# A four-layer graph network: the order of chunks in a tile of layer 0, and where the tile's end stands in the schedule

## The chip, the cores and the metric

The kernel runs on one core of a Trainium2 chip. Its time is the device time of one execution in microseconds (us); lower is better. The core has a matrix engine (TensorE, "PE" in the profile, with its weight loads as "PEld"), a vector engine (VectorE, "DVE"), a scalar engine (ScalarE, "ACT"), GpSimd ("POOL") and a queue that only issues transfers (SyncE, "SP"). Each engine takes its own instructions in a fixed order, and semaphores hold it where it needs another's result.

## The reference

Four graph layers run one after the other over 3125 nodes of 128 features and 100,000 edges, sorted by destination. Each layer's output is added to its input and normalized per node. Layer 0, which the change concerns most, is an attention over the edges that come into each node, with eight heads of 16 features, and with the node itself as one more neighbour:

```python
pre_edge = hP1[dst] + hP2[src] + zP3[edge_type]     # edge_type: one of 500 relations
logit_edge = _leaky(pre_edge) @ y_w                 # 128 -> 8 heads
alpha = ex / denom[dst_a]                           # softmax over a node's edges and itself
t_edge = hWh[src] + zWz[edge_type]
agg = jax.ops.segment_sum((alpha[:, :, None] * t).reshape(-1, D), dst_a, num_segments=n)
out = _leaky(agg + residual_weight * h)
```

Here hP1, hP2 and hWh are products of the node features with 128 x 128 weights, and zP3 and zWz are products of a table of 500 x 64 relation features. The self term also needs z_bar, the mean of the relation features of a node's edges. Layer 1 is a mean over neighbours with a small two-step network, layer 2 an attention with four heads and an edge bias, layer 3 an attention with typed nodes and edges.

## The kernel before

**Tiles, slots and chunks.** The nodes are sorted by degree and cut into 25 tiles of 128, one node per partition. A tile has CAP[t] edge slots per node (57 in tile 0, falling to 21), and `chunks(t)` cuts these into chunks of W = 8 slots and a shorter rest. A tile of the middle has five or four chunks. A prologue (`prologue`, L780 on) makes the node's own products hw and hq, and is issued for the next tile ahead of the last chunk of the present one.

**Two ways to do a chunk.** Both begin with eight gathers of neighbour rows from h_tab into a buffer hs (`gather`, L90, an indirect DMA on POOL; one gather brings one slot of all 128 nodes). hs has eight buffers.
- `gathered` (L819 on) also gathers eight rows of z_tab, the table of relation products, into a buffer zs, of which there are two. DVE adds zs to hs (L826), sums the relation features in halves (L814, L817) and adds them to the tile's sum (L828), after which zs is free. PE then forms the argument of the logits in PSUM (L799, L833), ACT applies the rectifier (L806), and PE multiplies with y_w (L808).
- `multiplied` (L838 on) gathers no zs. SP brings the relation numbers (L843), DVE makes one-hot matrices of them (L852), and PE multiplies these with the relation table (L854). ACT copies the result (zT, L856), PE forms the argument (L858, L860) and the value part (L866), which DVE adds to hs (L867). The relation features are summed from zT (L870, L874).

`by_matmul(t)` gives the first slots of the chunks that are multiplied. In a five-chunk tile they come as: multiplied, gathered, multiplied, gathered, gathered rest.

**The end of a tile.** `masked` (L881, L882) collects the logits of all chunks in lgs. `softmax` (L680 to L692) takes the maximum mx, the factor corr for what was summed earlier, the exponentials (ACT, L688) and their sum sm, and updates the running maximum m and the running sum l. `faded` (L697) scales the earlier sum ac. `spread` (L889, L814, L817, L891) multiplies the values of each chunk with the weights and sums them; when it is done with a chunk, that chunk's hs is free for a later gather. Then follow the self term, the output, the layer norm and the transfers out (L950 to L1008, with the scatter `put`, L93, on POOL). `softmax` is also used by layers 2 and 3, once per chunk there.

**Counts.** Layer 1 works with a table of how often each node is a neighbour of each other. `counts` (L562 to L645) makes this table from the edge lists on DVE, PE and ACT, during layer 0. It is a generator: after each chunk the loop takes some steps of it (`next(steps, None)`), so that the counts of all tiles are spread over layer 0. Only layer 1 reads the result (c_tab).

**What sets the order.** The program is written in plain order, and a scheduler puts the instructions of each engine in their final order. It takes what is ready by its own estimate of times, and among these prefers what has priority. Priority follows the order in the program, unless a block asks for more with `tc.high_priority(offset=...)`, which ranks the block that many places ahead. Pools decide when a buffer may be written again, in the order in which it was asked for: a gather into hs waits until the chunk eight chunks earlier was spread.

Of the kernel before, what the change touches and what calls it, by code (L numbers as in the profile page):

```python
# [8 lines left out]
F32 = mybir.dt.float32  # L9
# [3 lines left out]
AF = mybir.ActivationFunctionType  # L13
OP = mybir.AluOpType
AX = mybir.AxisListType
# [3 lines left out]
P = 128  # L19
N = 3125  # L20
NT = 25
# [6 lines left out]
W = 8  # L28
# [5 lines left out]
H = 8  # L34
# [6 lines left out]
CAP = [57, 42, 40, 39, 38, 37, 36, 35, 35, 34, 33, 33, 32, 31, 31, 30, 30, 29, 28, 28, 27, 26, 25, 24, 21]  # L41
assert len(CAP) == NT
OFF = [sum(CAP[:t]) for t in range(NT + 1)]
# [7 lines left out]
NB = [3] * 3 + [2] * (NT - 4) + [1]  # L51
CW = 512
NCW = -(-NP // CW)


def chunks(t):
    return [(s, min(W, CAP[t] - s)) for s in range(0, CAP[t], W)]
# [7 lines left out]
    return [(run[0][0], sum(run[-1]), run) for run in runs]  # L65


def by_matmul(t):

    full = CAP[t] // W  # L70
    n = (9 * CAP[t] + 10 * W) // (20 * W)
    return {i * full // n * W for i in range(n)}


@with_exitstack
def tile_gnn(ctx, tc, a, out):
    nc = tc.nc
    V, A, G, T = nc.vector, nc.scalar, nc.gpsimd, nc.tensor
# [400 lines left out]
    mask = late.tile([P, NS], F32, name="mask")  # L479
# [6 lines left out]
    with tc.tile_pool(name="srcp", bufs=1) as sp, tc.tile_pool(name="srcq", bufs=2, space=PSUM) as ps:  # L486
# [28 lines left out]
        for o in range(0, NS, P):  # L515
            n = min(P, NS - o)
# [158 lines left out]
    def softmax(pool, lg, n, heads, m, l, ex=None):  # L675


        ex = lg if ex is None else ex
        mx = pool.tile([P, heads], F32, name="mx")
        V.tensor_reduce(mx, lg.rearrange("p s h -> p h s"), AX.X, OP.max)  # L680
        mn = pool.tile([P, heads], F32, name="mn")
        V.tensor_max(mn, m, mx)
        corr = pool.tile([P, heads], F32, name="corr")
        V.tensor_sub(corr, m, mn)
        A.activation(corr, corr, AF.Exp)
        V.tensor_copy(m, mn)
        V.tensor_sub(lg, lg, mn.unsqueeze(1).to_broadcast([P, n, heads]))
        A.activation(ex, lg, AF.Exp)  # L688
        sm = pool.tile([P, heads], F32, name="sm")
        V.tensor_reduce(sm, ex.rearrange("p s h -> p h s"), AX.X, OP.add)  # L690
        V.tensor_mul(l, l, corr)
        V.tensor_add(l, l, sm)  # L692
        return corr

    def faded(acc, corr, heads):
        acch = acc.rearrange("p (h d) -> p h d", h=heads)
        V.tensor_mul(acch, acch, corr.unsqueeze(2).to_broadcast([P, heads, D // heads]))  # L697
# [56 lines left out]
    with tc.tile_pool(name="l0", bufs=2) as wp, tc.tile_pool(name="l0s", bufs=1) as sp, \  # L754
# [4 lines left out]
        m = sp.tile([P, NT, H], F32, name="m")  # L759
# [77 lines left out]
        def multiplied(hq, o, n, zbT, first, lg_ps):  # L837

            hs = wp.tile([P, W, HC], F32, name="hs", bufs=8)
            for s in range(n):  # L840
                gather(hs[:, s, :], h_tab, srcx[:, o + s:o + s + 1])
            rb = wp.tile([P, W * P], F16, name="rb")
            nc.sync.dma_start(rb[:, :n * P], rel_tab[o:o + n].rearrange("(o s) p -> o (s p)", o=1)  # L843
                              .to_broadcast([P, n * P]))
            zT = wp.tile([P, W * P], F32, name="zT")
            for s0 in range(0, n, 4):
                k = min(4, n - s0)
                cols = slice(s0 * P, (s0 + k) * P)
                oh = wp.tile([P, NK, 4 * P], BF16, name="oh")[:, :, :k * P]
                zps = ps1.tile([P, 4 * P], F32, name="zps")[:, :k * P]  # L850
                for i in range(NK):
                    V.tensor_scalar(oh[:, i], rb[:, cols], relid[:, i:i + 1], None, op0=OP.is_equal)  # L852
                    for k2 in range(2):
                        T.matmul(zps, zq[:, i, 2 * R * k2:2 * R * (k2 + 1)], oh[:, i], start=(i + k2 == 0),  # L854
                                 stop=(i == NK - 1 and k2 == 1))
                A.activation(zT[:, cols], zps, AF.Copy)  # L856
                pre = argument(hq, k)
                T.matmul(pre[:, :k], zw[:, :D], zT[:, cols], start=False, stop=False)  # L858
                for s in range(k):
                    T.matmul(pre[:, s, :], hs[:, s0 + s, :D], ident, start=False, stop=(s == k - 1))  # L860
                logits(pre, k, lg_ps[:, s0:s0 + k])
            for s0 in range(0, n, 3):
                k = min(3, n - s0)
                t_ps = ps1.tile([P, 3, HC - D], F32, name="t_ps")
                for s in range(k):
                    T.matmul(t_ps[:, s, :], zT[:, (s0 + s) * P:(s0 + s + 1) * P], zw[:, D:], start=True, stop=True)  # L866
                V.tensor_add(hs[:, s0:s0 + k, D:], hs[:, s0:s0 + k, D:], t_ps[:, :k])  # L867
            assert n == W
            zh = wp.tile([P, W // 2, P], F32, name="zh")
            V.tensor_add(zh, zT.rearrange("z (s p) -> z s p", p=P)[:, :W // 2],  # L870
                         zT.rearrange("z (s p) -> z s p", p=P)[:, W // 2:])
            halved(zh, W // 2, zbT if first else None)
            if not first:
                V.tensor_add(zbT, zbT, zh[:, 0])  # L874
            return hs

        def masked(lg_ps, hss, n, mk):

            lg = wp.tile([P, max(CAP), H], F32, name="lgs")
            for s0, w, hs in hss:  # L880
                V.tensor_add(lg[:, s0:s0 + w], lg_ps[:, s0:s0 + w], hs[:, :w, 2 * D:])  # L881
            V.tensor_add(lg[:, :n], lg[:, :n], mk.unsqueeze(2).to_broadcast([P, n, H]))  # L882
            return lg

        def spread(ac, hs, ex, n):

            val = hs[:, :n, D:2 * D]
            valh = val.rearrange("p s (h d) -> p s h d", h=H)
            V.tensor_tensor(valh, valh, ex.unsqueeze(3).to_broadcast([P, n, H, D // H]), op=OP.mult)  # L889
            halved(hs[:, :, D:2 * D], n)  # L890
            V.tensor_add(ac, ac, hs[:, 0, D:2 * D])  # L891
# [25 lines left out]
        for t in range(NT):  # L917
# [5 lines left out]
            lg_ps = ps1.tile([P, max(CAP), H], F32, name="lg")  # L923
            zbT = wp.tile([P, P], F32, name="zbT")
            hss = []
            mults = by_matmul(t)
            for s0, w in chunks(t):
                o = OFF[t] + s0
                if s0 + w == n and t + 1 < NT:

                    ahead = x_next, prologue(t + 1, x_next)
                if s0 in mults:
                    hs = multiplied(hq, o, w, zbT, s0 == min(mults), lg_ps[:, s0:s0 + w])
                else:
                    hs = gathered(hq, lambda s: srcx[:, o + s:o + s + 1], rel[:, o:o + w], w, za, lg_ps[:, s0:s0 + w])
                hss.append((s0, w, hs))

                done += n_steps * w / NS
                while done > 0:
                    next(steps, None)  # L940
                    done -= 1
            lg = masked(lg_ps, hss, n, mask[:, OFF[t]:OFF[t + 1]])
            corr = softmax(wp, lg[:, :n], n, H, m[:, t, :], l[:, t, :])
            faded(ac, corr, H)
            for s0, w, hs in hss:
                spread(ac, hs, lg[:, s0:s0 + w], w)


            zaT_ps = ps1.tile([P, P], F32, name="tp", tag="misc")
# [420 lines left out]
```

## Time and profile before

| | |
|---|---|
| Time, median of 3 runs | 4817.54 us (4814.24 to 4825.97) |
| Profiled execution, its own time | 5636.56 us |
| Its span in the profile | 5634.8 us |
| Mean granted TensorE clock | 0.619 of full |
| Busy in the span: POOL, DVE, PE, ACT | 54%, 53%, 36%, 16% |
| Preparation | 0 to about 204 us |
| Layer 0 | about 204 to 2850 us |
| Layer 1 | about 2850 to 3060 us |
| Layer 2 | about 3060 to 4400 us |
| Layer 3 | about 4400 to 5635 us |

The profile is of one execution, which was 819 us longer than the median of the runs without a profile. Durations come from it, and totals are to be set against its own time. A row of the groups names line, engine, operation, tile written and tiles read, count, busy time and mean duration, and then the idle time of the engine just before these instructions with what ended it. "issue" as a cause means that nothing in the profile shows a wait, and "remote" an update whose sender the trace doesn't tell.

### The profile page before, as it was taken

What the parts mean: (1) busy time and instruction counts of PE and PEld (TensorE: products, weight loads), DVE (VectorE), ACT (ScalarE), POOL (GpSimd) and SP (SyncE); (2) the same over time, 40 slices, a digit from 0 to 9 for tenths busy, and PEclk for the clock granted to TensorE, in tenths of its full rate; (3) what the DMA queues carried; (4) which work ended last, traced back from release to release, by engine and by line L of the source; (5) the groups of instructions that cost most, each with busy time, mean ns of one, the idle gap of its engine ahead of it and who ended that gap; (6) DMA issues with size and microseconds to landing.
All of it is one profiled execution on the core that took longest, in us unless ns stands there. A gap on an engine that the chain in (4) does not pass through costs nothing. (4 is left out here: it accounts for less than half of the span.)

```text
span 5634.8 us, 37936 instructions
## 1 busy us (share of the span) xinstructions
PE 2025.8 (36%) x10974; PEld 1311.2 (23%) x11061; DVE 2959.0 (53%) x6784; ACT 927.9 (16%) x2462; POOL 3069.7 (54%) x3137
## 2 busy tenths in 40 slices
PE   7164554556544555555564022222233100000000
PEld 5143433334333444334432010111111000000000
DVE  8354664555544655555432455555566354555555
ACT  1032222222222322222111011111111000000000
POOL 0545566454554445444503756666564476666665
PEclk9576766666676777776677555555555555555555
DMA  2423333332233333323343333333332233333322
GB/s 82 124 73 91 93 93 96 86 90 75 77 91 84 83 86 88 89 82 84 101 170 119 105 96 105 104 103 114 98 109 84 81 100 91 89 89 95 94 85 68
DMA packets 220244, 530.70 MB, mean 94 GB/s; under 512 B 65689, under 2 KB 112460, under 8 KB 215385
## 3 DMA queue, kind: packets, MB, share of 16 engines
q0 software_dynamic: 147968, 437.97, 27.6%
q1 hardware_dynamic: 72024, 89.90, 4.9%
q8 instruction: 94, 1.54, 0.1%
q14 instruction: 158, 1.29, 0.1%
HBM read 457.09 MB, written 70.63 MB: 94 GB/s over the span
## 5 line engine op out<-in xcount | busy, mean ns | idle before, releaser
L90 POOL DMA_INDIRECT hs<-h_tab,srcx x821 | 880.3, 1072 | 666.2 <-issue 534.7
L90 POOL DMA_INDIRECT kv<-kv_tab,pay_sb x821 | 783.6, 954 | 423.9 <-issue 241.1
L90 POOL DMA_INDIRECT kv<-ktv_tab,pay_sb x821 | 780.2, 950 | 336.0 <-issue 256.1
L90 POOL DMA_INDIRECT zs<-z_tab,rel x445 | 458.0, 1029 | 451.6 <-DVE az L828 141.6
L706 DVE TENSOR_REDUCE u<-msg 128x128 f32<-128x1024 f32 (+4 forms) x228 | 384.3, 1686 | 114.5 <-remote 61.6
L808 PE MATMUL lg<-yw,low 128*128 128x8 f32 x1642 | 243.5, 274 | 126.2 <-ACT low L806 72.2
L634 PE MATMUL c_ps<-c_ohs,c_ohd 128*128 128x128 bf16 x1300 | 139.5, 264 | 406.3 <-issue 193.9
L808 PEld LDWEIGHTS lg<-yw,low 128*128 128x128 f32 x1642 | 235.5, 218 | 173.0 <-ACT low L806 107.1
L1315 DVE TENSOR_TENSOR qk<-kv,qp 128x1024 f32<-128x1024 f32 (+4 forms) x114 | 126.5, 1110 | 279.4 <-DMA kv<-ktv_tab,pay_sb 257.4
L559 DVE TENSOR_TENSOR c_ohs<-c_ends,c_up 128x1024 bf16<-128x1024 bf16 (+4 forms) x178 | 113.2, 637 | 296.1 <-remote 251.0
L612 ACT ACTIVATE c_oha<-c_oha,srclo 128x50 bf16<-128x50 bf16 (+2 forms) x821 | 201.4, 327 | 355.6 <-DVE c_oha L608 270.1
L854 PE MATMUL zps<-oh,zq 128*128 128x512 bf16 x677 | 237.7, 466 | 49.4 <-DVE oh L852 21.4
L702 DVE TENSOR_TENSOR msg<-kv,ex 128x1024 f32<-128x1024 f32 (+4 forms) x228 | 249.3, 1105 | 0.0
L866 PE MATMUL t_ps<-zw,zT 128*128 128x136 f32 x752 | 153.3, 340 | 212.9 <-DVE hs L867 128.2
L1163 DVE TENSOR_TENSOR qk<-kv,qp 128x1024 f32<-128x1024 f32 (+4 forms) x114 | 126.1, 1107 | 183.2 <-DMA kv<-kv_tab,pay_sb 175.6
L634 PEld LDWEIGHTS <-c_ohd 128*128 128x128 bf16 x1300 | 114.0, 118 | 431.8 <-issue 333.0
L799 PE MATMUL pre<-identb,hq 128*128 128x512 bf16 (+3 forms) x645 | 203.3, 414 | 5.0 <-issue 4.1
L636 ACT ACTIVATE c_sb<-c_ps 128x512 bf16<-128x512 f32 (+1 forms) x175 | 96.3, 550 | 653.8 <-remote 441.9
L717 PE MATMUL tp<-ident,xk 128*128 128x128 f32 x100 | 43.6, 436 | 432.7 <-DVE xk L1231 131.2
L806 ACT ACTIVATE low<-pre 128x512 f32<-128x512 f32 (+1 forms) x215 | 123.1, 574 | 406.3 <-remote 140.3
L826 DVE TENSOR_TENSOR hs<-hs,zs 128x2112 f32<-128x2112 f32 (+7 forms) x67 | 132.6, 1979 | 102.9 <-issue 43.8
L866 PEld LDWEIGHTS t_ps<-zw,zT 128*128 128x128 f32 x752 | 130.1, 234 | 239.2 <-DVE hs L867 137.5
(398 smaller groups left out, 5183.8 us busy)
## 6 DMA issues: line engine op xcount, KB each, us to landing
c_tab<-c_sb SPq DMA_DIRECT2D x25, 768.0 KB
cs<-c_tab SPq DMA_DIRECT2D x6, 3200.0 KB
hs<-h_tab,srcx POOLq DMA_INDIRECT x821
kv<-kv_tab,pay_sb POOLq DMA_INDIRECT x821
kv<-ktv_tab,pay_sb POOLq DMA_INDIRECT x821
rb<-rel_tab SPq DMA_DIRECT2D x47, 256.0 KB
zs<-z_tab,rel POOLq DMA_INDIRECT x445
h_tab<-h SPq DMA_DIRECT2D x25, 132.0 KB
```

The source lines that it names most:

```text
L90: return G.indirect_dma_start(out=dst, out_offset=None, in_=table, in_offset=indirect(idx), **kw)
L612: A.activation(oha[:, s, 0, :], oha[:, s, 1, :], AF.Copy, scale=srclo[:, o:o + 1])
L634: T.matmul(cps[:, j * P:(j + 1) * P], ohd[:, b // 2, :, b % 2], ohs[:, b // 2, :, b % 2], start=(i == 0), stop=(i == nb - 1))
L702: V.tensor_tensor(msg[:, :n, :].rearrange("p s (h d) -> p s h d", h=heads), val.rearrange("p s (h d) -> p s h d", h=heads), ex.unsqueeze(3 ...
L706: V.tensor_reduce(u, msg[:, :n, :].rearrange("p s d -> p d s"), AX.X, OP.add)
L799: T.matmul(pre[:, :k], hq[:, i, :], identb.unsqueeze(1).to_broadcast([P, k, P]), start=(i == 0), stop=False)
L808: T.matmul(lg_ps[:, s, :], low[:, s, :], yw8, start=True, stop=True)
L826: V.tensor_add(hs[:, :n], hs[:, :n], zs[:, :n, :HC])
L854: T.matmul(zps, zq[:, i, 2 * R * k2:2 * R * (k2 + 1)], oh[:, i], start=(i + k2 == 0), stop=(i == NK - 1 and k2 == 1))
L866: T.matmul(t_ps[:, s, :], zT[:, (s0 + s) * P:(s0 + s + 1) * P], zw[:, D:], start=True, stop=True)
L1163: V.tensor_mul(qk[:, :n], kv[:, :n, :D], qp.unsqueeze(1).to_broadcast([P, n, D]))
L1315: V.tensor_mul(qk[:, :n], kv[:, :n, :D], qp.unsqueeze(1).to_broadcast([P, n, D]))
```

## The change

1. `by_matmul(t)` becomes `in_order(t)`. As many chunks are multiplied as before, now always the first ones by slot number, and the list alternates between gathered and multiplied chunks so that a multiplied one is last. The gathered chunks are taken from the end of the tile, so the short rest comes first. A five-chunk tile becomes: gathered rest, gathered, multiplied, gathered, multiplied. The prologue of the next tile is still issued ahead of the last chunk.
2. `softmax` is split. `weights` does what the values need, with the exponentials of the logits ahead of that of corr. `rest` does the copy of m, the sum sm and the update of l. In layer 0 `rest` comes behind the spreads; layers 2 and 3 still call both together, through `softmax`.
3. The tile's end, from `masked` to `rest`, is in a block with a priority of AHEAD = 600 places.
4. zbT, the sum of the multiplied relation features, is begun by the chunk with slot 0, which is the first multiplied one in the new order too.

```diff
--- before.py
+++ after.py
@@ -51,6 +51,7 @@
 NB = [3] * 3 + [2] * (NT - 4) + [1]
 CW = 512
 NCW = -(-NP // CW)
+AHEAD = 600
 
 
 def chunks(t):
@@ -65,11 +66,14 @@
     return [(run[0][0], sum(run[-1]), run) for run in runs]
 
 
-def by_matmul(t):
-
-    full = CAP[t] // W
+def in_order(t):
+
+
     n = (9 * CAP[t] + 10 * W) // (20 * W)
-    return {i * full // n * W for i in range(n)}
+    mult = [(s, w, True) for s, w in chunks(t)[:n]]
+    rest = [(s, w, False) for s, w in chunks(t)[n:]][::-1]
+    k = len(mult) + len(rest)
+    return [(mult if (i + 1) * n // k > i * n // k else rest).pop(0) for i in range(k)]
 
 
 @with_exitstack
@@ -675,6 +679,12 @@
     def softmax(pool, lg, n, heads, m, l, ex=None):
 
 
+        corr, rest = weights(pool, lg, n, heads, m, l, ex)
+        rest()
+        return corr
+
+    def weights(pool, lg, n, heads, m, l, ex=None):
+
         ex = lg if ex is None else ex
         mx = pool.tile([P, heads], F32, name="mx")
         V.tensor_reduce(mx, lg.rearrange("p s h -> p h s"), AX.X, OP.max)
@@ -682,15 +692,18 @@
         V.tensor_max(mn, m, mx)
         corr = pool.tile([P, heads], F32, name="corr")
         V.tensor_sub(corr, m, mn)
-        A.activation(corr, corr, AF.Exp)
-        V.tensor_copy(m, mn)
         V.tensor_sub(lg, lg, mn.unsqueeze(1).to_broadcast([P, n, heads]))
         A.activation(ex, lg, AF.Exp)
-        sm = pool.tile([P, heads], F32, name="sm")
-        V.tensor_reduce(sm, ex.rearrange("p s h -> p h s"), AX.X, OP.add)
-        V.tensor_mul(l, l, corr)
-        V.tensor_add(l, l, sm)
-        return corr
+        A.activation(corr, corr, AF.Exp)
+
+        def rest():
+            V.tensor_copy(m, mn)
+            sm = pool.tile([P, heads], F32, name="sm")
+            V.tensor_reduce(sm, ex.rearrange("p s h -> p h s"), AX.X, OP.add)
+            V.tensor_mul(l, l, corr)
+            V.tensor_add(l, l, sm)
+
+        return corr, rest
 
     def faded(acc, corr, heads):
         acch = acc.rearrange("p (h d) -> p h d", h=heads)
@@ -923,14 +936,14 @@
             lg_ps = ps1.tile([P, max(CAP), H], F32, name="lg")
             zbT = wp.tile([P, P], F32, name="zbT")
             hss = []
-            mults = by_matmul(t)
-            for s0, w in chunks(t):
+            todo = in_order(t)
+            for i, (s0, w, mult) in enumerate(todo):
                 o = OFF[t] + s0
-                if s0 + w == n and t + 1 < NT:
+                if i + 1 == len(todo) and t + 1 < NT:
 
                     ahead = x_next, prologue(t + 1, x_next)
-                if s0 in mults:
-                    hs = multiplied(hq, o, w, zbT, s0 == min(mults), lg_ps[:, s0:s0 + w])
+                if mult:
+                    hs = multiplied(hq, o, w, zbT, s0 == 0, lg_ps[:, s0:s0 + w])
                 else:
                     hs = gathered(hq, lambda s: srcx[:, o + s:o + s + 1], rel[:, o:o + w], w, za, lg_ps[:, s0:s0 + w])
                 hss.append((s0, w, hs))
@@ -939,11 +952,14 @@
                 while done > 0:
                     next(steps, None)
                     done -= 1
-            lg = masked(lg_ps, hss, n, mask[:, OFF[t]:OFF[t + 1]])
-            corr = softmax(wp, lg[:, :n], n, H, m[:, t, :], l[:, t, :])
-            faded(ac, corr, H)
-            for s0, w, hs in hss:
-                spread(ac, hs, lg[:, s0:s0 + w], w)
+
+            with tc.high_priority(offset=AHEAD):
+                lg = masked(lg_ps, hss, n, mask[:, OFF[t]:OFF[t + 1]])
+                corr, rest = weights(wp, lg[:, :n], n, H, m[:, t, :], l[:, t, :])
+                faded(ac, corr, H)
+                for s0, w, hs in hss:
+                    spread(ac, hs, lg[:, s0:s0 + w], w)
+                rest()
 
 
             zaT_ps = ps1.tile([P, P], F32, name="tp", tag="misc")
```

## The prediction

> **What bounds the kernel now.** I read the page first, for the costliest rows.
>
> ```profile
> PE 2025.8 (36%) x10974; PEld 1311.2 (23%) x11061; DVE 2959.0 (53%) x6784; ACT 927.9 (16%) x2462; POOL 3069.7 (54%) x3137
> ...
> L90 POOL DMA_INDIRECT hs<-h_tab,srcx x821 | 880.3, 1072 | 666.2 <-issue 534.7
> ...
> L90 POOL DMA_INDIRECT zs<-z_tab,rel x445 | 458.0, 1029 | 451.6 <-DVE az L828 141.6
> ```
>
> Both rows belong to layer 0, and POOL issues them one after the other. The timeline of POOL shows the step in an undisturbed stretch: 0.95 us busy, 0.30 between, one gather each 1.25 us. Layer 0 has 821 + 445 + 25 indirect DMAs (the 25 are L93), so its floor on POOL is 1291 x 1.25 = 1614 us. It lasts from about 204 to 2850 us: 2646 us. The view by stretches says that no engine is full there:
>
> ```profile
> 204.00:1200.00 996.00, 514.34 (x3228) 375.77 (x3255) 502.98 (x1239) 251.75 (x685) 570.24 (x540) 0.68 0.34 91
> 1200.00:1400.00 200.00, 111.38 (x621) 78.92 (x628) 89.34 (x235) 47.75 (x136) 102.04 (x97) 0.65 0.30 81
> 1400.00:2850.00 1450.00, 791.23 (x4844) 559.68 (x4884) 767.46 (x2201) 366.95 (x969) 723.95 (x705) 0.70 0.31 85
> ```
>
> Columns: length, busy us of PE, PEld, DVE, ACT and POOL, then clock, DMA share, GB/s. So layer 0 is bound by waits between engines. Those of POOL, layer 0 only:
>
> ```profile
> POOL hs L90 <- issue: 534.7, 773, 38.4
> POOL zs L90 <- DVE az L828: 141.6, 14, 19.3
> ...
> POOL x_tab L93 <- DVE x L735: 79.5, 7, 36.0
> ```
>
> "issue" here is mostly one long wait a tile plus 0.30 per gather: 773 waits, 534.7 us, so about 773 x 0.30 = 232 of stepping and 300 of real waiting. What ends a long one is seen where tile 9's end meets tile 10's fourth chunk, POOL above, DVE below:
>
> ```profile
> 1507.89 0.95 POOL L90 DMA_INDIRECT zs<-z_tab,rel  x1 [19.10 <-DVE az L828]
> 1532.62 5.77 POOL L90 DMA_INDIRECT hs<-h_tab,srcx  x1 [23.78 <-issue]
> ```
>
> ```profile
> 1497.71 2.35 DVE L826 TENSOR_TENSOR hs<-hs,zs 128x2112 f32<-128x2112 f32 x1
> ...
> 1516.32 0.69 DVE L881 TENSOR_TENSOR lgs<-lg,hs 128x64 f32<-128x64 f32 x5
> ...
> 1524.10 1.51 DVE L593 TENSOR_REDUCE c_pos<-c_inc 128x32 f32<-128x800 f32 x1
> 1525.53 0.16 DVE L692 TENSOR_TENSOR l<-l,sm 128x8 f32<-128x8 f32 x1
> 1525.60 1.22 DVE L889 TENSOR_TENSOR hs<-hs,lgs 128x1024 f32<-128x1024 f32 x1
> ...
> 1531.60 0.28 DVE L891 TENSOR_TENSOR az<-az,hs 128x128 f32<-128x128 f32 x1
> ```
>
> The hs gather starts 0.7 us after L891 of the old tile's first chunk ends: it had waited for an hs buffer. Between the L826 add of the NEXT tile's first gathered chunk (1497.7) and that release (1531.9) DVE does the tile end mixed with count work (L559, L589, L593). All long gaps of 1 us or more add up in layer 0 to some 898 us: hs 425, zs 320, the rest put and x.
>
> The profiled execution took 5636.6 us, 819 more than the median 4817.5. Many waits in it end "remote" (ACT c_sb L636 441.9 us, DVE c_ohs L559 251.0), so they are partly the recording's. Were all 819 us in layer 0, it would really last 1827; were they spread evenly, 2261. I take 2050, so 2050 - 1614 = 436 us of real POOL waiting (range 210 to 650). All sums below are differences made on profile durations and put on the median.
>
> **What the Trainium skill says.** "Perfetto Trace Analysis", Optimization Strategy: a bubble that repeats on the engine that should be saturated can mean too few buffers for the next tile. The trace agrees: 38.4, 26.4, 23.8, 34.1, 24.4 us on consecutive tiles, each at the ninth hs buffer. The same page, DMA Instruction — SWDGE (GPSIMD): the recorded end of a GpSimd DMA is the end of descriptor generation, and the data lands later. No row here gives that landing time, so it is part of an 8.5 us allowance below. "SBUF — State Buffer", the box on SWDGE: a DVE operation in a two-port mode can keep GpSimd from writing descriptors. The 5.77 us gather above fits, beside DVE's spread; nothing here proves it. DVE's amount of work does not change, so I give it nothing.
>
> **The change, part by part.**
>
> Order of chunks: a five-chunk tile goes from M G M G r to r G M G M (M multiplied, G gathered, r the short gathered rest). Gathers stay 821 + 445, multiplied chunks 47 of 114, DVE work of tiles 1 to 23 goes 1236 to 1243 us. Nothing is bought in work; only positions move. I laid both programs' queues side by side. The tile's own last gather now stands 35 to 55 gathers ahead of the first one that needs its buffers (16 to 49 before). That would pay, but in both queues the spread still stands on DVE behind the L826 add of the next tile's gathered chunk, so the cover counts from THAT chunk's last gather. In gathers, tiles 1 to 12: before 8 8 8 30 8 16 8 8 1 8 8 41; after 11 2 16 17 8 3 0 12 9 8 8 9. Four-chunk tiles 13 to 19: before 41 to 49; after 35 29 40 39 4 38 37.
>
> DVE from that gate to the release: mean 18.5 us before (6.4 of it counts), 16.1 after (4.8). The scheduler still mixes counts in: tile 8 goes from 23.0 to 30.1 us, 15.6 of it counts.
>
> Price per tile: max(0, gate-to-release + 8.5 - cover x 1.25). Tile 8: before 23.0 + 8.5 - 10 = 21.5 (the trace shows 26.4, so the model has about the right size); after 30.1 + 8.5 - 15 = 23.6. Tile 6: 23.2 + 8.5 - 20 = 11.7, after 25.3 + 8.5 - 3.8 = 30.0. Tile 3: 22.7 + 8.5 - 10 = 21.2, after 23.3 + 8.5 - 20 = 11.8. Tile 12: 27.7 + 8.5 - 51 is below 0, after 26.4 + 8.5 - 11 = 23.7. Done gather by gather, largest wait of each tile: hs 235 before, 263 after; zs (same rule, released by L828) 110 before, 94 after. Sum 345 against 357: +12 us. The allowance is my estimate; at 3 us the difference is -6, at 16 us +60. Scaled to the 436 us above (x 436/345): +15, from -8 to +76.
>
> weights/rest: the m copy (0.163), sm (0.618), two operations on l (0.157 each) go behind the spreads, about 1.1 us of DVE a tile off the release, 27 us over 25 tiles if each tile waits there; this is already in the 16.1. Exp of corr (206 ns) behind the other exp: under 0.2 us a tile. For layers 2 and 3 these are the same operations in another order, and u L706 and msg L702 fill DVE there beside kv gathers: 0, at most 228 x 0.16 = 36 us either way, if each chunk waited for it.
>
> high_priority by 600: no instruction added. Counts are put behind; they feed layer 1 only, at 2850, so hidden; uncovered they can cost up to one tile's share, 22 us. Queued behind a tile end placed early on DVE are the next chunk's L826 and L852, and so PE and the zs release. SP's rb loads go with their chunks: 47 before and after, none on the path.
>
> Sum: 4817.5 + 15 (stalls), and a few us for delayed count and put work (a guess between 0 and 22, taken as 7): 4840.
>
> **Rivals.**
> A, faster: the tile end really stops binding. If the spread comes out ahead of the next tile's L826 in time as well as in the queue, half of the hs waits go: 425/898 x 436 = 206, half 103, and 27 more from the shorter end: about 4690. For: the repeating bubble, the tile's own slack of 35 to 55 gathers (44 to 69 us). Against: the gate in the queue. It decides if the next tile's first gathered chunk lands before the last multiplied one of this tile is through PE.
> B, no change: DVE, PE and POOL are each so near the tile period that a wait taken from hs comes back at zs or x_tab: 4817.
> C, slower by more: the four-chunk tiles, which wait nowhere by my sum before, now have their buffers released late, and early-placed tile ends hold up L826. With a step of 1.0 us a gather instead of 1.25, less cover, the same sum gives 732 against 578, +154; half of it +77: 4895, up to 4970.
>
> **How the numbers follow.** A measurement of this kernel tells 0.3%, 14 us, from no change. Forecast, 4810 to 4895 with 4840 as its middle: 0.42 (faster 0.02, same 0.10, slower 0.30). A, 4690 to 4803: 0.30, faster. B: 0.08 (0.02 faster, 0.04 same, 0.02 slower). C, 4895 to 4970: 0.20, slower. Together faster 0.34, same 0.14, slower 0.52. The range leaves out the ends of A and C: 4705 to 4950; the forecast's own is 4810 to 4895.
>
> **What would show it.** Right: POOL hs waits per tile of 15 to 30 us still there in tiles 3 to 11, new ones in tiles 12 to 16 and 19, zs waits ended by L828 a little smaller, the L826 of the next tile ahead of L881 in DVE's timeline. Rival A: hs waits fall under 200 us and the tile period shrinks evenly. C: DVE waits ahead of L826 and x_tab grow. Wrong about layers 2 and 3: their stretches change length by over 20 us. What would make it all wrong: real waits that the recording hides, since it is 17% longer than the runs.

## The result

The changed kernel takes 4879.56 us (median of 4 runs, 4875.56 to 4883.56) where the kernel before takes 4818.69 (4 runs beside it). The ratio is 1.0125, with a 95% interval of 1.0107 to 1.0142: 61 us slower. The forecast was 4840, so its direction was right and its size too small by almost a factor of three (+22 of +61).

The profile of the changed kernel has a span of 4878.6 us, near its runs. That of the kernel before, on which the prediction rests, had 5634.8. So the kernel before was profiled once more (run before_again below); this second profile has 4814.1 us and is the one to compare with. From here on, "before" in comparisons of traces is this second profile. In some groups of runs the kernel before takes 5589 to 5643 us, without a profile too, for a reason that is open, so each result stands beside the time of the kernel before in its own group, and only groups with about 4819 us are compared with the result above.

Where the time goes is seen from when layers 1, 2 and 3 begin. The lines are from the view by tile (the matmuls of layer 1, the gathers of layers 2 and 3), with minimum, median and maximum duration in ns and then the first and last start in us. Kernel before, second profile:

```profile
L1113 PE MATMUL y_ps<-cs,u x513: 219/379/631, 2319.1 to 2457.8; 128*128 128x512 bf16 x146, 128*128 128x128 bf16 x25
L90 POOL DMA_INDIRECT kv<-kv_tab,pay_sb x821: 941/947/1616, 2508.8 to 3607.2; - x165
L90 POOL DMA_INDIRECT kv<-ktv_tab,pay_sb x821: 941/947/1142, 3692.4 to 4783.5; - x165
```

The changed kernel (its lines stand 4 to 16 further down):

```profile
L1129 PE MATMUL y_ps<-cs,u x513: 219/379/631, 2386.3 to 2524.7; 128*128 128x512 bf16 x146, 128*128 128x128 bf16 x25
L94 POOL DMA_INDIRECT kv<-kv_tab,pay_sb x821: 940/946/1578, 2576.3 to 3674.3; - x165
L94 POOL DMA_INDIRECT kv<-ktv_tab,pay_sb x821: 940/946/1111, 3758.0 to 4848.0; - x165
```

Layer 1 begins 67 us later, and the two steps after that are 190 and 1182 us long against 190 and 1184. All of the loss is in layer 0; the reordered softmax of layers 2 and 3 costs nothing.

The groups of the page that answer to those shown before the prediction, changed kernel:

```profile
PE 1915.6 (39%) x10963; PEld 1273.4 (26%) x11061; DVE 2923.6 (60%) x6784; ACT 921.7 (19%) x2462; POOL 3167.7 (65%) x3137
...
L94 POOL DMA_INDIRECT hs<-h_tab,srcx x821 | 937.1, 1141 | 389.0 <-issue 269.8
...
L94 POOL DMA_INDIRECT zs<-z_tab,rel x445 | 498.2, 1120 | 194.1 <-issue 123.8
L839 DVE TENSOR_TENSOR hs<-hs,zs 128x2112 f32<-128x2112 f32 (+5 forms) x67 | 132.9, 1984 | 566.2 <-DMA zs<-z_tab,rel 480.6
```

and the second profile of the kernel before:

```profile
L90 POOL DMA_INDIRECT hs<-h_tab,srcx x821 | 919.0, 1119 | 380.9 <-issue 323.8
...
L90 POOL DMA_INDIRECT zs<-z_tab,rel x445 | 487.7, 1096 | 181.8 <-issue 124.2
L826 DVE TENSOR_TENSOR hs<-hs,zs 128x2112 f32<-128x2112 f32 (+7 forms) x67 | 132.9, 1984 | 498.5 <-DMA zs<-z_tab,rel 344.3
```

The same gathers are busy 18 + 11 us longer: no gather was added, but one takes 1141 and 1120 ns in the mean instead of 1119 and 1096. The idle time in front of them grew by 8 + 12 us. DVE sits 68 us longer in front of its add of zs, where it waits for the gathers of zs, and all that is queued on DVE behind this add waits too.

That suggests an account of layer 0 by POOL's timeline. From the first hs gather to the last hs or zs gather, the time is: 0.95 us for each of about 1311 DMAs and the small gaps between them (together 1642 us before and 1638 in the changed kernel), plus the **waits** (gaps of 1 us and more), plus the **excess** (what each of these DMAs lasts beyond 0.95 us). The **tail** is from the end of the last gather to the first matmul of layer 1.

| us | waits | excess | tail |
|---|---|---|---|
| before | 183 | 210 | 79 |
| changed | 204 | 244 | 95 |
| difference | +22 | +34 | +16 |

These three give 72, the small rest takes back some 4, and the start of layer 1 moved by 67. Half of the loss is thus not waiting at all, but gathers that last longer. The longest of the changed kernel, with the DVE rows at its end:

```profile
354.10 15.54 POOL L94 DMA_INDIRECT hs<-h_tab,srcx  x1 [5.32 <-issue]
```

```profile
367.94 0.28 DVE L904 TENSOR_TENSOR az<-az,hs 128x128 f32<-128x128 f32 x1
368.14 0.68 DVE L827 TENSOR_TENSOR hs<-hs 128x512 f32<-128x512 f32 x1
368.74 0.96 DVE L702 TENSOR_REDUCE sm<-lgs 128x8 f32<-128x456 f32 x1
```

During all of the 15.54 us DVE runs the spread. The gather ends at 369.64 us, 0.90 us after the start of the first DVE instruction behind it. If the excess of every DMA is laid over the DVE instructions that run from its start to 0.9 us before its end, 75 us of it before and 115 in the changed kernel fall on the spread; the add of zs (L826, L839 in the changed kernel) has 69 and 70. So the growth is the spread's.

### The profile page after: what moved, and what is told of

Same layout as the page of the kernel before. It is cut to its first block, busy times and chain, and to the rows that moved or that the text cites. A ratio compares the mean times of both kernels' runs of the same rounds, so it can differ in the third digit from the quotient of the medians.

```text
span 4878.6 us, 37948 instructions
## 1 busy us (share of the span) xinstructions
PE 1915.6 (39%) x10963; PEld 1273.4 (26%) x11061; DVE 2923.6 (60%) x6784; ACT 921.7 (19%) x2462; POOL 3167.7 (65%) x3137
## 4 chain that ended last, share of the span: by engine, by line
POOL 24%; issue 13%; DVE 6%; PE 5%; DMA 3%; ACT 1%; DVEq 0%; another core or an unknown queue 0%; SPq 0%; POOLq 0%; ACTq 0%
POOL kv L94 23%; PE y_ps L1129 2%; DVE msg L715 1%; DMA kv<-kv_tab,pay_sb 1%; DVE u L719 1%; DMA kv<-ktv_tab,pay_sb 1%; PE p_ps L1249 1%; DVE qk L1179 1%; PE e_ps L1257 1%; DVE qk L1331 1%; PE p_ps L1144 0%; POOL xqb L94 0%; POOL out L97 0%; POOL ktv_tab L97 0%; PE tp L730 0%
## 5 line engine op out<-in xcount | busy, mean ns | idle before, releaser
L94 POOL DMA_INDIRECT hs<-h_tab,srcx x821 | 937.1, 1141 | 389.0 <-issue 269.8
L94 POOL DMA_INDIRECT zs<-z_tab,rel x445 | 498.2, 1120 | 194.1 <-issue 123.8
L839 DVE TENSOR_TENSOR hs<-hs,zs 128x2112 f32<-128x2112 f32 (+5 forms) x67 | 132.9, 1984 | 566.2 <-DMA zs<-z_tab,rel 480.6
L846 PE MATMUL pre<-ident,hs 128*128 128x128 f32 x890 | 180.2, 354 | 221.8 <-DVE hs L839 221.8
L867 PE MATMUL zps<-oh,zq 128*128 128x512 bf16 x666 | 209.4, 421 | 56.9 <-DVE oh L865 47.9
L846 PEld LDWEIGHTS pre<-ident,hs 128*128 128x128 f32 x890 | 163.2, 259 | 239.0 <-DVE hs L839 229.8
L879 PE MATMUL t_ps<-zw,zT 128*128 128x136 f32 x752 | 142.5, 319 | 123.2 <-DVE hs L880 117.3
L819 ACT ACTIVATE low<-pre 128x512 f32<-128x512 f32 (+2 forms) x215 | 122.6, 574 | 332.5 <-PE pre L846 198.8
L1249 PE MATMUL p_ps<-wqkv,xkT 128*128 128x384 f32 x200 | 160.4, 904 | 46.6 <-ACT xkT L732 46.6
L725 ACT ACTIVATE qp<-xqb 128x128 f32<-128x128 f32 x50 | 13.9, 280 | 811.3 <-DVE qk L1331 544.9
```

The source lines that it names most:

```text
L94: return G.indirect_dma_start(out=dst, out_offset=None, in_=table, in_offset=indirect(idx), **kw)
L1249: T.matmul(p_ps, xkT, wqkv[:, k, :], start=(k == 0), stop=(k == NTY - 1))
```

## The experiments

**before_again.** The kernel before, unchanged.

> The kernel before, profiled once more, because its first profile is 819 us longer than its runs while that of the changed kernel is not. If the recording was at fault, this profile's span is near 4820 us, "remote" ends no long waits, and it can be compared with the changed kernel's: layer 0 there takes 2143 us and layers 2 and 3 together 2293 us. My theory (the loss is in layer 0) expects layer 0 some 60 us shorter here, about 2080, and layers 2 and 3 the same within 10. The rival (the changed order of the exponentials in layers 2 and 3) expects those layers 50 to 60 us shorter here and layer 0 equal.

Span 4814.1 us, layer 0 shorter by 67 us than in the changed kernel, the later layers equal within 3 us. The theory's place for the loss holds, the rival on layers 2 and 3 falls. It does not show that the recording was at fault in the first profile, since runs without one have taken as long.

**order_only, prio_only, split_only.** One part of the change alone, in the kernel before.

```diff
 order_only:  -    mults = by_matmul(t)            +    todo = in_order(t)
 prio_only:   +    with tc.high_priority(offset=AHEAD):   # masked, softmax, faded, spread
 split_only:  +    corr, rest = weights(...)   ...   rest()   # behind the spreads
```

> Only the new order of the chunks; softmax and the tile's end as before, no priority. Theory (the chunk order takes cover away from the hs buffers): slower by most of the 61 us, 4860 to 4890. Rival P (the priority places tile ends ahead of the next chunk's work): within 15 us of 4819. Rival S (the split softmax): within 15 us of 4819.

> Only the priority of 600 for the tile's end; order of chunks and softmax as before. Theory (chunk order): within 20 us of 4819, on either side. Rival P: slower by 40 to 60, 4860 to 4880. Rival S: within 15 us of 4819.

> Only the split of softmax (weights, rest behind the spreads in layer 0, the exponential of the logits first in all layers). Theory: faster by 0 to 25 us, 4794 to 4819, since it shortens the way to the release by 1.1 us a tile. Rival S (in layers 2 and 3 the reordered softmax delays something 114 times a layer): slower by 40 to 60. Rival P: within 15 us of 4819.

| | us (before: 4819.2) | ratio (95%) | waits | excess | tail |
|---|---|---|---|---|---|
| order_only | 4912.3 | 1.0195 (1.0167 to 1.0223) | 250 | 233 | 83 |
| prio_only | 4817.9 | 0.9995 (0.9983 to 1.0008) | 115 | 280 | 85 |
| split_only | 4803.9 | 0.9964 (0.9953 to 0.9976) | 174 | 210 | 79 |

The order of the chunks is the part that costs, 93 us alone and mostly in waits (+68); this is more than its theory allowed (4860 to 4890). The split gains 15 and the priority comes out at nothing, both within the theory's ranges, so the rivals P and S fall. How the priority comes out at nothing is instructive: 67 us less waiting, 69 us more excess. Tile ends that come early do free their hs buffers earlier, but gathers last longer. POOL in the kernel with the priority alone, from the timeline:

```profile
1631.97 1.00 POOL L91 DMA_INDIRECT hs<-h_tab,srcx  x1 [0.30 <-issue]
1633.28 11.03 POOL L91 DMA_INDIRECT hs<-h_tab,srcx  x1 [0.30 <-issue]
1644.61 0.95 POOL L91 DMA_INDIRECT hs<-h_tab,srcx  x1 [0.30 <-issue]
```

and DVE of the same kernel in these 11 us, the timeline's last rows:

```profile
1641.98 0.28 DVE L892 TENSOR_TENSOR az<-az,hs 128x128 f32<-128x128 f32 x1
1642.18 0.28 DVE L818 TENSOR_TENSOR hs<-hs 128x128 f32<-128x128 f32 x1
1642.38 0.90 DVE L591 TENSOR_TENSOR c_inc<-c_inc,c_oh 128x725 f32<-128x725 f32 x1
1643.21 0.28 DVE L892 TENSOR_TENSOR az<-az,hs 128x128 f32<-128x128 f32 x1
1643.41 1.41 DVE L594 TENSOR_REDUCE c_pos<-c_inc 128x29 f32<-128x725 f32 x1
```

One gather stood from 1633.28 to 1644.31 us, while DVE went without a gap through the spread and one product of the counts (L591): multiplications and additions that read two operands from SBUF. It ended 0.9 us after the start of the first DVE instruction that reads only one (L594, at 1643.41). The long gathers of the changed kernel look alike: its zs gather at 1641.93 lasts 10.28 us and ends 0.9 us after the first reduction behind the spread.

**four_old and five_old.** The changed kernel, with the old order kept in a part of the tiles.

```diff
 def in_order(t):
+    if len(chunks(t)) < 5:      # four_old; five_old has >= 5
+        at = {i * (CAP[t] // W) // n * W for i in range(n)}
+        return [(s, w, s in at) for s, w in chunks(t)]
```

> The changed kernel, but tiles with fewer than five chunks (12 to 24) keep the old order of chunks. In the trace of the changed kernel the spreads of tiles 0 to 10 end up to 16 us earlier than before, and all of the loss comes with tiles 11 to 14. Theory (the four-chunk tiles lose slack because a multiplied chunk comes last there): most of the loss is gone, 4800 to 4830. Rival (the loss belongs to the five-chunk tiles and only shows later): 4865 to 4885.

> The other half: tiles 0 to 11 keep the old order, tiles 12 to 24 have the new one; priority and split as in the changed kernel. Theory (four-chunk tiles): still slower than before by 45 to 75 us, 4865 to 4895. Rival (five-chunk tiles): 4800 to 4830.

They ran where the kernel before takes 5643 us: 5763.3 (ratio 1.0199, 1.0167 to 1.0230) and 5631.5 (0.9974, 0.9959 to 0.9989). The absolute times of the expectations don't apply there, so both were repeated.

> Once more, for a chip where the kernel before takes about 4819 us as in the first comparisons: on the chip of the last four runs it took 5643 us, with long waits that end "remote", and there this kernel was 2.0% slower. The changed kernel with the old order in tiles 12 to 24 (fewer than five chunks). Theory (four-chunk tiles lose slack): 4800 to 4830. Rival (the loss belongs to the five-chunk tiles 2 to 11): 4865 to 4885. The last runs, on the other chip, speak for the rival.

> The other half, on a chip where the kernel before takes about 4819 us: old order in tiles 0 to 11, new one in tiles 12 to 24. Theory (four-chunk tiles): 4865 to 4895. Rival (five-chunk tiles): 4800 to 4830; the last runs, where it came out 0.3% faster than before, speak for it.

Beside 4815.2 us of the kernel before, four_old_b takes 4850.9 (1.0068, 1.0049 to 1.0086) and five_old_b 4843.5 (1.0062, 1.0046 to 1.0079). Neither the theory nor the rival holds: the two kernels lose 36 and 28 of the 61 us. The account by POOL shows that these are not halves of one thing: waits 183 and 165 (183 before, 204 changed), excess 246 and 247 (210 and 244), tail 84 and 94 (79 and 95). The excess is whole in each of them, so it does not hang on where the new order stands; both have the priority and the split. The waits of the changed kernel come only with the new order in all tiles. The tail's extra 15 us come with the new order in the last tiles. That the loss seems to come with tiles 11 to 14 in the trace was thus a wrong reading: it shows where a lead and a lag change places, not whose loss it is. Beside 5643 us only the first of the two lost; why they differ there stays open.

**after_stt.** The spread's operations as another DVE instruction.

```diff
-  V.tensor_tensor(valh, valh, ex, op=OP.mult); V.tensor_add(v, v, v2) ...
+  V.scalar_tensor_tensor(valh, valh, 1.0, ex, op0=OP.mult, op1=OP.mult)
+  V.scalar_tensor_tensor(v, v, 1.0, v2, op0=OP.mult, op1=OP.add) ...
```

> The changed kernel with the spread's multiplication and additions written as scalar_tensor_tensor with a factor of 1.0: the same sums by another DVE instruction. In both traces gathers that are under way during the spread's plain additions almost never end before those do (0.1 to 0.3 ends per us, against 0.7 during the count work), and gathers last 244 us longer in layer 0 than 0.95 us each, against 210 before. Theory (DVE's plain fp32 additions in SBUF hold up the gathers): the excess falls to 100 to 150 us and the kernel gains 40 to 110 us: 4770 to 4840. Rival (gathers are merely slow while the released buffers' semaphores pass, or for another reason that doesn't hang on the instruction): 4870 to 4890, the excess as it was.

> The changed kernel with scalar_tensor_tensor in the spread, on a chip where the kernel before takes about 4819 us. Theory (plain fp32 additions of DVE in SBUF hold up the gathers): gather excess 100 to 150 us in layer 0 instead of 244, time 4770 to 4840. Rival (the excess doesn't hang on the instruction): 4870 to 4890, excess as it was. On the other chip the excess was 161 us and the time 1.7% above before, but there is no run of the changed kernel there to set it against.

Where the kernel before takes 5643 us it took 5747.9 (1.0169, 1.0145 to 1.0193); in the comparable place 4877.5 (1.0131, 1.0114 to 1.0148), with an excess of 242 us and waits of 203. The rival's numbers hold: nothing changed. But this instruction reads two operands from SBUF as well, so the run excludes only that the choice between these two instructions matters. (By the account used here the excess beside 5643 us was 202 us, not the 161 of the second expectation, and its ends per us come out higher: 0.32 and 0.19 for the additions of the spread in the changed kernel, 0.57 and 0.32 before, against 0.9 to 1.0 for the counts. They point the same way.)

**no_prio.** The changed kernel without the priority.

```diff
-            with tc.high_priority(offset=AHEAD):
-                lg = masked(...)
+            lg = masked(...)
```

> The changed kernel without the priority: new order of chunks and split softmax. If the parts add up, this is the order alone (4912) less the split's 15 us: about 4897, and the priority is worth 17 us in the new order though it was worth nothing in the old one. If the split's gain hangs on the old order: 4905 to 4915. If priority makes no difference in either order: 4875 to 4885.

> New order and split softmax without the priority, on a chip where the kernel before takes about 4819 us. Parts that add up: about 4897. The split worth nothing in this order: 4905 to 4915. Priority without effect: 4875 to 4885. On the other chip it came out 0.3% faster than before, which none of the three had.

5629.1 us (0.9970, 0.9958 to 0.9982) beside 5643, and 4855.4 (1.0086, 1.0069 to 1.0103) beside 4815.2: waits 232, excess 218, tail 79. None of the three expectations holds. In the new order the split is worth some 53 us (1.0195 to 1.0086) where it was worth 15 in the old one; why so much is open. The priority costs 19 on top (1.0086 to 1.0125). Just as in the old order it turns waits (-27) into excess (+26), and it adds 16 us of tail. In the changed kernel 62 us pass from the last gather to the last put of the layer, in the kernel before 47; the multiplied chunk at the end of the last tile alone doesn't do that, since no_prio has it too.

**after_reduce and split_reduce.** The three halving additions of the spread become one reduction with one operand, in the changed kernel and in split_only.

```diff
-            halved(hs[:, :, D:2 * D], n)
-            V.tensor_add(ac, ac, hs[:, 0, D:2 * D])
+            V.tensor_reduce(hs[:, 0, :D], val.rearrange("p s d -> p d s"), AX.X, OP.add)
+            V.tensor_add(ac, ac, hs[:, 0, :D])
```

> The changed kernel with the spread's three halving additions (two SBUF operands each) replaced by one tensor_reduce (one operand) into columns of hs that are dead by then. DVE works about 0.3 us longer per chunk, 35 us over layer 0. Theory (additions with two SBUF operands keep GpSimd from making descriptors): the gathers' excess over 0.95 us falls from 244 us to about 140 to 190, and the time from 4880 to 4800 to 4865, the longer DVE work included. Rival (long gathers come from something else at the tile's end, as the release itself): excess 230 to 260, and the time 4880 to 4915.

> The same replacement in the kernel before with only the split of softmax, which took 4804. Theory: excess from 210 to about 120 to 160 and 4740 to 4800. Rival: excess 200 to 220, 4804 to 4835. If the excess falls and the time does not, the waits for hs buffers have taken its place: 4795 to 4815 with waits of 1 us or more up from 174.

after_reduce takes 4794.1 us beside 4819.0 (0.9943, 0.9926 to 0.9961): 85 us less than the changed kernel and faster than the kernel before, although DVE works longer. Excess 190 (from 244), waits 169 (from 204). split_reduce takes 4756.0 (0.9866, 0.9849 to 0.9883), with an excess of 181 (from 210) and waits of 160 (from 174). In the first the excess comes out at the upper end of the theory's range and the time below it; in the second the excess fell less than expected, but the time is in its range. The waits did not take the place of the excess, they fell too, by 35 and 14 us; so the gain is not all excess. The new reduction on DVE, from the groups of after_reduce:

```profile
L903 DVE TENSOR_REDUCE hs<-hs 128x128 f32<-128x1024 f32 (+7 forms) x114 | 201.0, 1778 | 0.0
```

It takes 1.78 us a time where the additions for 8 slots took 0.68 + 0.42 + 0.28. No gather of layer 0 lasts over 3.4 us in after_reduce, against 15.5 in the changed kernel. While a reduction and a gather run together, 0.82 gathers end per us, against 0.32 (L827) and 0.19 (L830) beside the additions of the changed kernel.

**lock_probe.** The disputed cost alone, in the kernel before, in layer 3.

```diff
+                if t % 3 < 2 and w == W:
+                    for _ in range(3):
+                        V.tensor_add(probe[t % 3], parts[-1][:, :4, D:], probe[t % 3])   # probe[0] SBUF, probe[1] PSUM
```

> The disputed cost by itself, in layer 3, where DVE idles some 500 us and gathers follow each other without waits. Three more DVE additions of 128x512 fp32 per full chunk, of no use to the output: in tiles 0, 3, 6... with the other operand and the result in SBUF, in tiles 1, 4, 7... with these in PSUM, none in the remaining tiles. Theory (two SBUF operands hold up the gathers): gathers of the first kind of tile are longer by 1 to 2 us per chunk or more, those of the second as in the third, about 0.95 us. Rival: the three kinds of tile alike within 2%.

The two kinds of additions in the view by tile of this kernel, and POOL's timeline beside three additions of the first kind:

```profile
L1343 DVE TENSOR_TENSOR probe_s<-kv,probe_s x102: 647/680/693, 3693.0 to 4796.8; 128x512 f32<-128x512 f32 x102
```

```profile
L1343 DVE TENSOR_TENSOR probe_p<-kv,probe_p x87: 664/684/697, 3773.9 to 4738.5; 128x512 f32<-128x512 f32 x87
```

```profile
3692.66 0.95 POOL L90 DMA_INDIRECT kv<-ktv_tab,pay_sb  x1 [0.30 <-issue]
3693.91 1.35 POOL L90 DMA_INDIRECT kv<-ktv_tab,pay_sb  x1 [0.30 <-issue]
3695.57 0.95 POOL L90 DMA_INDIRECT kv<-ktv_tab,pay_sb  x1 [0.31 <-issue]
```

Both kinds take 0.68 us. Of 846 indirect DMAs in layer 3 (821 gathers and the 25 scatters of the output), 26 last longer than 1.2 us, and all 26 run beside an addition with both operands in SBUF (the longest 2.09 us); beside those with an operand in PSUM the longest is 1.08, and in layer 3 before it is 1.14. The size was overestimated: layer 3 has 18.2 us of excess against 4.2 before, which is 0.41 us for each of 34 chunks instead of 1 to 2.

The second kind of addition also writes to PSUM, so this run alone doesn't tell the operand from the place of the result. The kernel's own instructions do. In the trace before and in that of the changed kernel, take every indirect DMA that starts while a TENSOR_TENSOR or TENSOR_REDUCE of DVE has 0.45 us or more to go, and ask if it lasts over 1.1 us. Where this instruction reads two operands from SBUF (the spread, the add of zs, c_inc, c_oha and others), 241 of 284 do. Where one operand is in PSUM and the result goes to SBUF (hs<-hs,t_ps; qk<-kv,qp; msg<-kv,ex; c_ohs, c_ohd and c_ohb, which read c_up), 0 of 564. For reductions it is 0 of 763. So two operands in SBUF are what holds a gather. It can be held as long as such instructions follow each other without a break, and the count work that reads c_up, a table in PSUM, lets it go: in none of the 219 gathers of layer 0 over 1.5 us in these two traces does a reduction, or one of these instructions with an operand in PSUM, start in the time between, until 1 us before the gather's end.

**split_prio_reduce and split_reduce_all.** The priority added to split_reduce; and split_reduce with the relation sums as reductions too.

```diff
 split_reduce_all:
-            halved(zs[:, :, HC:], n)
-            V.tensor_add(za, za, zs[:, 0, HC:])
+            V.tensor_reduce(zs[:, 0, :R], zs[:, :n, HC:].rearrange("p s d -> p d s"), AX.X, OP.add)
+            V.tensor_add(za, za, zs[:, 0, :R])          # and zbT from zT in the same way
```

> Old order of chunks, split softmax, priority for the tile's end and the reduction in the spread: the changed kernel with one-operand sums and without the new order. The priority alone was worth 0, with 67 us less waiting and 69 us more excess. Theory (that excess was the spread's additions): now a part of the waiting is won for good, excess 190 to 230, waits 90 to 130, 4715 to 4750. Rival (any dense run of DVE work costs the gathers the same): 4750 to 4775, as without the priority. It also prices the order in this surrounding: after_reduce took 4794.

> split_reduce, with the relation sums (zs in gathered chunks, zT in multiplied ones) made by one-operand reductions too, in place of halving additions with two SBUF operands. Theory (additions with two SBUF operands hold up gathers wherever they stand): excess from 181 to about 140 to 165, 4715 to 4745. Rival (only the long run at the tile's end matters): excess 170 to 190, and 4750 to 4775 with the longer DVE work.

split_prio_reduce takes 4772.2 us beside 4822.3 (0.9904, 0.9878 to 0.9930), excess 169, waits 170, tail 91. The theory's time and waits fail here: with the additions gone the priority still gains nothing (4756.0 without it), and the waits that fell by 67 in prio_only do not fall. split_reduce_all takes 4713.2 (0.9777, 0.9755 to 0.9800): 2.2% faster than the kernel before and the fastest of all. Its time is better than the theory's range, but not by its mechanism: the excess fell by 9 us only (172), the waits by 39 (121). The relation sums had little excess to give; the add of zs, which no run touched, still has 72 of the 172 us. One reduction in place of several additions makes gated buffers free sooner, or the schedule came out better; no run tells these apart.

**split_prio.** All parts except the order.

```diff
-            lg = masked(...); corr = softmax(...); faded(...); spread(...)
+            with tc.high_priority(offset=AHEAD):
+                lg = masked(...); corr, rest = weights(...); faded(...); spread(...); rest()
```

> Everything of the change except the order of chunks: split softmax and priority in the old order. It closes the table of the three parts. If the order's price doesn't hang on the other two parts, this takes 4879 less some 90: 4785 to 4795. If split and priority simply add up in the old order (-15 and 0): 4800 to 4810, the order then costs 70 to 80 beside them. If the priority costs the same 24 us as it did in the new order beside the split (4855 to 4880): 4820 to 4835.

It ran where the kernel before takes 5589 us: 5621.2 (1.0051, 1.0024 to 1.0079). That can't be set against the changed kernel, which was not run there. The order's price with both other parts in place is therefore open; with the reduction in place as well it is about 20 us (0.9943 against 0.9904).

## Why the prediction was wrong

**What binds: right in kind, in part in place.** Waits for hs buffers at the end of a tile, behind the L826 add of the next tile, are in both traces, and the new order has them in other tiles. For the release of tile 8 the working had 21.5 us before and 23.6 after; the second profile before and the changed one show 19 and 18. For tile 12 it had nothing before and 23.7 after; measured 0 and 23. For tile 6 it had 11.7 and 30.0; measured 8 and 16. Tile 3's 21.2 and 11.8 became 22 and 0. But of the new waits that it announced for tiles 12 to 16 and 19 only that of tile 12 came; for the others no hs wait reaches 4 us. So covers counted from the queues, with durations from the profile, find some of the tiles, and are off by up to 14 us in these four.

**The sum of the waits: near, in part by luck.** Forecast +15, measured +22. But the forecast had hs +28 and zs -16 ahead of its scaling, and measured are +7 (135 to 142) and +15 (47 to 62); the two errors cancel. The levels were too high (345 us of hs and zs before, measured 183), probably because a wait that moves all later gathers makes the following ones shorter, and the sum counted each on its own; no run shows this. The layer's real waiting, taken as 436 us, is 393 if the excess is counted with it. The floor of 1614 us left out the 25 gathers of x and so was 28 us low (1642).

**"DVE's amount of work does not change, so I give it nothing": this step failed.** It gave the long gathers no price because no instruction is added. Measured: +34 us of excess, more than the waits themselves (+22). What counts is not how much DVE does but what POOL does meanwhile, and how long two-operand instructions follow each other without a break. Before, the spread came in pieces with count work between them: unbroken stretches of 5 us and more make up 61 of its 255 us, and 49 us of it fell into waits of POOL, where it holds up nothing. In the changed kernel such stretches make up 234 of 248 us, one for nearly every tile, and 38 us fall into waits. The gathers over 5 us are 5 before and 12 after. In prio_only it is 218 of 249 and 32, so the priority is enough for both; in order_only 173 of 251, but 59 in waits, with 22 us more excess. So longer unbroken stretches go with more excess; how much of it is theirs, and how much the waits that no longer cover the spread, no run tells apart.

The prediction had seen the 5.77 us gather and read the box on two-port modes, which is about other instructions than those of the spread. In the same page of the Trainium skill, "SBUF — State Buffer", section "Who interferes with whom", a nearer case is stated: a DVE instruction with two SBUF inputs contends with a GpSimd instruction that reads SBUF. The runs agree for indirect DMAs, which take their row numbers from a tile in SBUF: 241 of 284 against 0 of 564, and 54 us less excess with a one-operand reduction. The same section also says that tensor_tensor has no two-port mode and did not stall a DMA in an earlier measurement. For the indirect DMAs of this case it does, and the measurement decides.

**"a few us for delayed count and put work (... taken as 7)": mis-sized.** The tail grew by 16 us, with the multiplied chunk at the end of the last tile and the priority together: either alone adds about 5 us or less (83 in order_only and 85 in prio_only against 79). The 91 of split_prio_reduce, in the old order, is not explained by this.

**The split: right in direction.** It was counted inside the waits; alone it is worth 15 us, within the 27 that the working gave it at most; the 53 in the new order are beyond that working. Layers 2 and 3 at 0: right, within 2 us.

**"they are partly the recording's": not borne out.** Executions without a profile took as long. The estimate of layer 0 (2050 us, measured 2115 from 204 to 2319) was near by luck.

**Rivals.** A (faster, because the tile end stops binding) had a true core: the priority does take 67 us of waiting away in the old order. It missed the same step. B (no change) fell with the interval of the ratio, but its thought was near what prio_only did: the hs waits fell by 95 us, of which 27 came back at zs and x_tab and 69 as excess. C (four-chunk tiles only) was wrong in its place: the kernels with the new order in one kind of tile lose in both. Its signs did come, longer waits of DVE ahead of L826 (+68 us) and of the last puts (part of the tail), with a time just below its range from 4895.

## What to carry to other kernels

When a wait is shortened, ask what the waiting engine would have run into had it not waited: here the instructions that release the buffer are the ones that hold up the gathers, so the priority won 67 us of waits and lost 69 of excess. Two ways out are in these kernels: one operand of a long DVE instruction in PSUM, or one reduction in place of several additions. Count the time of a queue of transfers as steps, waits and excess over the undisturbed duration, since a gain in one that comes back in another shows only in such a table. And where a trace shows a few instructions that take five to ten times their median, find what runs beside them before costing a change of order at zero.

## What was not expected of the hardware

An indirect DMA of GpSimd, 0.95 us when undisturbed, lasted up to 18.5 us in prio_only and 15.5 us in the changed kernel while DVE ran operations with two SBUF operands back to back. A break of one instruction with an operand in PSUM, or with one operand in all, was enough: the gather then ended some 0.9 us later.
